# A three-layer decoder on one core: biases of the first two tiles on TensorE, the other two put off, adapters from two tables, twelve of sixteen parts by squares from the fifth batch

## The chip, the cores and the metric

The kernel runs on one core of a Trainium2 chip. The metric is the device time of one execution in microseconds (us). Five engines work beside one another, each with its own queue that it runs in order: PE (TensorE, matrix multiplies and transposes), DVE (VectorE), ACT (ScalarE), POOL (GpSimd) and SP (SyncE, which here only issues DMAs).

## The reference

`x` is 8 batches of 512 rows of 256 values; everything is 32-bit floating point. Three layers follow one another, each ended by `x = layernorm(x + layer(x))`.

```python
# 1: linear attention (16 heads of 16) and an MLP
xn = layer_norm(x, ln1_w, ln1_b)
q, k, v = (xn @ w.T + b for w, b in ((q_w, q_b), (k_w, k_b), (v_w, v_b)))   # split over heads
q, k = elu(q) + 1, elu(k) + 1
kv = einsum('bhnd,bhne->bnde', k, v)             # per row n: a sum over the 16 heads
attn = einsum('bhnd,bnde->bhne', q, kv) / einsum('bhnd,bnd->bhn', q, k.sum(axis=1))[..., None]
x = x + attn @ o_w.T + o_b
x = x + gelu(layer_norm(x, ln2_w, ln2_b) @ fc_w.T + fc_b) @ proj_w.T + proj_b      # hidden width 1024
# 2: cross-attention, 16 heads of 64, over 512 rows of context of width 128
attn = softmax((x @ Wq) @ (ctx @ Wk).T / 8);  out = (attn @ (ctx @ Wv)) @ Wo + bo
# 3: a base layer and one of 8 adapters for each batch
losses = mean((relu(x @ W_enc[n] + b_enc[n]) @ W_dec[n] + b_dec[n] - x) ** 2)      # per batch and n
a = connected_idx[argmin(losses)]
out = x @ W_base + b_base + relu(x @ W_down[a] + b_down[a]) @ W_up[a] + b_up[a]
```

The sums `kv` and `attn` of layer 1 run over heads or over 16 features within one row, so they are no matrix multiplies: they are elementwise products and reductions.

## The kernel before, in words

**A planner writes the order.** The program first lists tasks (`task(engine, took, due, emit, reads, writes, ...)`). Each has an engine, an estimated duration in ns, a due time, and values that it reads and writes. `others=` names engines that may take it instead after a wait; `two=True` says that on DVE it reads two SBUF operands, and `alone()` then makes it exclude POOL's elementwise work in the plan. `play()` then goes through a planned time and, at each step, gives every free engine the ready task with the earliest due time whose buffers are free (`rooms`, `roomy`). The result is a fixed instruction order for PE, ACT, DVE, POOL and for SP's DMAs. Due times are in units of PACE = 3200 ns; batch b's cross-attention is due from 64·b PACE on. A planned time orders the work and sets no wait on the chip, where semaphores alone hold an instruction back.

**Layer 1** (`linear_attention`, `tile_attention`) goes by tiles of 128 rows, four to a batch (c = 0 to 3). For each tile: norm (DVE statistics L388, POOL power L402, DVE scale L410), transposes and `turn_tile` (scale and bias, DVE L460), projection to q, k and v on PE (`project`, L511), the bias of q and k added by DVE in PSUM (L519), that of v on its way to SBUF (L527), exponential on ACT (L523, L524), k and q (DVE L537, L549). Then four products k·v of 128x1088 (L559, POOL, or DVE), each summed by DVE (L568); four products q·kv (L582, POOL, or DVE) and their sums (L591); division, output projection (L632), second norm. Batch 0 runs its MLP tile by tile (`mlp_by_tiles`, L712 and L687); later batches run layer 1 some two batches ahead of their cross-attention, in `WINDOWS` of due times. `FIRST` holds the due times of batch 0's four tiles.

**Layer 2** (`cross_attention`, `attend`) goes by pairs of heads (8) and halves of the rows (2): 16 parts to a batch. Batch 0 does its eight pairs for tiles 0 and 1 first, and for tiles 2 and 3 after that, so that it can start when two tiles are through. A part has four score tiles of 128x512 (L847), maxima (DVE L854), exponential (ACT L862), scaling by 1/sum (POOL L873 or ACT L871), transposition of the probabilities, and the weighting of v (`weigh`, L929). The transposition has two forms. By PE: 16 transposes of 128x128 into PSUM (L893) and four copies out (ACT L372 or DVE L374). By squares, for the parts listed in `BLOCKED`: DVE transposes each 128x512 tile in 32x32 squares (L883, four to a part) into `blk`, and SP issues 16 DMAs (`place`, L913) that move the squares within SBUF into `pT`. There is one buffer of its own for `blk` and one for `pT`, and one more of each that lies over two of layer 1's four product buffers (`prods`). Probabilities before transposition have seven buffers (`p`).

**Layer 3** (`ffn`): base bias added to x by POOL (L377 with `bbase`, four tiles), encoders L973 and decoders L1076, squared errors on ACT (L1093), the adapter chosen by nine small DVE operations (`choose`, L1102 to L1115), five indirect DMAs issued by POOL (L1001: two for W_down, one each for b_down, W_up, b_up), the middle product (L1019), relu with bias (L1023), then by tiles: b_up added by POOL (L377 with `bu`), base and up products in one PSUM group (L1038, L1039), added by DVE (L1045), norm, output by SP (L1060, L1066).

## Time and profile before

| | |
|---|---|
| median of 3 runs | 1677.8 us (1677.01 to 1680.26) |
| the profiled execution: its time, and its span from first to last instruction | 1677.12 us, 1675.3 us |
| busy: PE, DVE, ACT, POOL | 1569.5, 1320.5, 1084.0, 1075.2 us |
| mean granted PE clock over the span | 0.972 |
| first scores of cross-attention (L847) | 103.73 us after the start |
| parts transposed by squares | 61 of 128 (976 DMAs of L913) |

The profile's times are counted from the first instruction of the span. A group's line gives engine, operation, tiles written and read, how many, busy time and mean time of one. A window's line gives the busy time of each engine in that stretch, the PE clock granted, and what the DMA engines did. In a timeline an entry shows start and duration, and in brackets how long the engine had been idle and what it had waited for.

### The profile page before, as it was taken

The numbers are of one execution on the slowest core, as the hardware profiler recorded it, in microseconds if no ns is written. First come the engines' busy times: TensorE is split into PE (matmuls) and PEld (weight loads), VectorE is DVE, ScalarE is ACT, GpSimd is POOL, SyncE is SP. The second block draws the span as 40 slices with busy tenths as digits, with TensorE's granted clock in tenths as the row PEclk, the third lists the DMA queues.
The fourth block names the chain that finished last, engine by engine and source line by source line (L and its number), as shares of the span: only waits on it lengthen the run. The fifth ranks groups of instructions, "written<-read, shape, count | busy, mean of one in ns | idle before, by whom it ended". The sixth has DMA issues, their size and how long they took to land.

```text
span 1675.3 us, 23902 instructions
## 1 busy us (share of the span) xinstructions
PE 1569.5 (94%) x7856; PEld 935.4 (56%) x7856; DVE 1320.5 (79%) x2261; ACT 1084.0 (65%) x2359; POOL 1075.2 (64%) x881
## 2 busy tenths in 40 slices
PE   4489999999999999999998999989999899999996
PEld 2366666664665555565565565655566554654562
DVE  7987886798889898979976797868969566776554
ACT  1147776678676787678756677657766567646643
POOL 6955886686678697669565794758938241544243
PEclk8689999999999999999999999999999999999998
DMA  8000000022113211221113121221112322333301
GB/s 267 1 1 1 1 1 0 8 54 58 33 34 88 52 26 38 53 75 51 48 29 89 46 52 30 59 79 28 51 35 55 88 72 68 80 100 91 91 7 32
DMA packets 159003, 86.68 MB, mean 52 GB/s; under 512 B 18336, under 2 KB 156192, under 8 KB 158880
## 3 DMA queue, kind: packets, MB, share of 16 engines
q1 hardware_dynamic: 157472, 83.06, 18.4%
q0 software_dynamic: 1408, 2.10, 0.6%
q8 instruction: 63, 1.03, 0.3%
q14 instruction: 60, 0.49, 0.1%
HBM read 16.93 MB, written 4.19 MB: 13 GB/s over the span
## 4 chain that ended last, share of the span: by engine, by line
PE 74%; DVE 10%; SPq 4%; issue 3%; ACT 3%; POOL 3%; DMA 2%; POOLq 0%; DVEq 0%; ACTq 0%
PE sc L847 12%; PE bank L929 12%; PE bank L687 7%; PE bank L662 6%; PE bank L945 5%; PE bank L793 5%; PE bank L893 5%; PE bank L511 4%; SPq L913 4%; PE bank L973 3%; PE bank L800 3%; PE bank L1076 3%; PE bank L809 3%; DVE o L591 2%; ACT p L862 2%
## 5 line engine op out<-in xcount | busy, mean ns | idle before, releaser
L862 ACT ACTIVATE p<-sc,nmax 128x512 f32<-128x512 f32 x512 | 348.1, 689 | 111.3 <-DVE nmax L854 88.6
L873 POOL TENSOR_SCALAR p<-p,rinv 128x512 f32<-128x512 f32 x284 | 204.5, 731 | 325.6 <-DVE rinv L867 316.5
L854 DVE TENSOR_REDUCE nmax<-sc 128x2 f32<-128x1024 f32 x256 | 304.9, 1213 | 82.7 <-PE sc L847 82.0
L559 POOL TENSOR_TENSOR prods<-k,v 128x1088 f32<-128x1088 f32 x119 | 297.5, 2523 | 59.8 <-DVE k L537 32.6
L847 PE MATMUL sc<-kT,qT 64*128 64x512 f32 x1024 | 265.5, 627 | 5.5 <-ACT p L862 4.3
L582 POOL TENSOR_TENSOR prods<-q,kv 128x1088 f32<-128x1088 f32 x95 | 237.4, 2519 | 37.3 <-DVE kv L568 25.6
L568 DVE TENSOR_REDUCE kv<-prods 128x68 f32<-128x1088 f32 x128 | 162.3, 1273 | 10.9 <-POOL prods L559 10.5
L893 PEld LDWEIGHTS bank<-ident,p 128*128 128x128 f32 x1072 | 121.7, 141 | 80.4 <-issue 45.7
L591 DVE TENSOR_REDUCE o<-prods 128x68 f32<-128x1088 f32 x128 | 160.6, 1271 | 4.5 <-POOL prods L582 4.5
L871 ACT ACTIVATE p<-p,rinv 128x512 f32<-128x512 f32 x228 | 155.5, 730 | 3.2 <-DVE rinv L867 2.7
L893 PE MATMUL bank<-ident,p 128*128 128x128 f32 x1072 | 150.3, 277 | 2.6 <-ACT qT L804 1.1
L847 PEld LDWEIGHTS sc<-kT,qT 64*128 64x128 f32 x1024 | 88.7, 190 | 109.6 <-issue 77.2
L929 PE MATMUL bank<-prods,v 128*64 128x256 f32 x1008 | 127.9, 397 | 16.0 <-DMA prods<-blk 14.7
L883 DVE STREAM_TRANSPOSE blk<-p 128x512 f32<-128x512 f32 x184 | 121.9, 689 | 25.7 <-POOL p L873 11.0
L929 PE MATMUL bank<-pT,v 128*64 128x256 f32 x1040 | 128.0, 388 | 4.0 <-DMA prods<-prods 2.1
L793 PE MATMUL bank<-x1T,Wq 128*128 128x512 f32 (+1 forms) x288 | 124.1, 554 | 1.0 <-DVE x L1045 0.5
L945 PE MATMUL bank<-Wo,oT 128*128 128x256 f32 x512 | 121.1, 382 | 0.0
L687 PE MATMUL bank<-projT,h 128*128 128x256 f32 x512 | 119.1, 383 | 1.3 <-ACT h L723 1.3
L687 PEld LDWEIGHTS bank<-projT,h 128*128 128x128 f32 x512 | 95.3, 190 | 26.0 <-issue 9.2
L945 PEld LDWEIGHTS bank<-Wo,oT 128*128 128x128 f32 x512 | 94.8, 190 | 26.5 <-issue 12.1
L929 PEld LDWEIGHTS bank<-prods,v 128*64 128x64 f32 x1008 | 70.2, 141 | 70.6 <-issue 29.6
L372 ACT COPY oT<-bank 128x256 f32<-128x256 f32 x100 | 37.2, 372 | 110.2 <-PE bank L929 109.7
(142 smaller groups left out, 2859.1 us busy)
## 6 DMA issues: line engine op xcount, KB each, us to landing
prods<-blk SPq DMA_DIRECT2D x480, 64.0 KB, 2.1
pT<-blk SPq DMA_DIRECT2D x256, 64.0 KB, 2.1
prods<-prods SPq DMA_DIRECT2D x176, 64.0 KB, 2.1
pT<-prods SPq DMA_DIRECT2D x64, 64.0 KB, 2.1
x<-in_x SPq DMA_DIRECT2D x7, 512.0 KB, 6.5
out<-x SPq DMA_DIRECT2D x7, 512.0 KB, 3.4
ctx<-in_ctxT SPq DMA_DIRECT2D x8, 256.0 KB, 3.1
fcT<-in_fcT SPq DMA_DIRECT2D x1, 1024.0 KB
```

The costliest lines, as they stand in the source:

```text
L559: (nc.gpsimd if e == "pool" else nc.vector).tensor_tensor(pr.t.rearrange("p (d e h) -> p d e h", d=DSPLIT, h=H1), k.t[:, s : s + DSPLIT, : ...
L582: (nc.gpsimd if e == "pool" else nc.vector).tensor_tensor(pr.t.rearrange("p (h e d) -> p h e d", h=DSPLIT, d=D1), q.t[:, s : s + DSPLIT, : ...
L591: nc.vector.tensor_reduce(o.t[:, s : s + DSPLIT, :], pr.t.rearrange("p (h e d) -> p h e d", h=DSPLIT, d=D1), AX.X, ALU.add)
L687: nc.tensor.matmul(ps.t[:, :C], of(f, c), projT[:, f, :], start=f == fs[0], stop=f == fs[-1])
L793: nc.tensor.matmul(ps_q.t[:, :n], Wq[:, kc, cols], x1T.t[:, kc, rows], start=kc == 0, stop=kc == KC - 1)
L847: nc.tensor.matmul(ps.t[:, i, :], qT.t[rows, c * P : (c + 1) * P], kT.t[rows, :], start=True, stop=True)
L854: lambda: nc.vector.tensor_reduce(nmax.t, ps.t, AX.X, ALU.max, negate=True), [(ps, 0)], [(nmax, 0)],
L862: lambda i=i, p=p: nc.scalar.activation(p.t, ps.t[:, i, :], AF.Exp, bias=nmax.t[:, i : i + 1], accum_out=ssum.t[:, i : i + 1]),
L873: nc.gpsimd.tensor_scalar(p.t, p.t, rinv.t[:, i : i + 1], 1.0, ALU.mult, ALU.mult)
L893: nc.tensor.transpose(bank.t[:, m * P : (m + 1) * P], p.t[:, m * P : (m + 1) * P], ident)
L929: nc.tensor.matmul(to, v2.t[:, m, cols], of, start=m == 0, stop=m == NT - 1)
L945: nc.tensor.matmul(ps.t[:, :C], oT.t[:, c * P : (c + 1) * P], Wo[:, pr, :], start=pr == prs[0], stop=pr == prs[-1])
```

## The change

Four edits go together.

1. *Opening.* For tiles 0 and 1 of batch 0 (`EARLY`) the biases of q, k and v come from a third matmul of one row (`ones` times `bqkv`) in the same PSUM group; the DVE bias adds are gone, and ACT copies v. Their `kv` lies in a PSUM tile of the scores' room instead of SBUF, and their q·kv products are DVE's alone and no longer exclude POOL in the plan. Tiles 2 and 3 get later due times (`FIRST`), and their k·v products may not be planned before 65 and 75 us (`HOLD`). `turn_tile` goes to ACT first. The bias loads are issued behind the three weight loads.
2. *Adapters.* The host lays W_down, b_down, W_up, b_up and the base bias in two tables, so two gathers stand for five. Two rows that are always one carry b_up and the base bias through the up product; the eight POOL additions of each batch are gone. `choose` has seven operations instead of nine. In the last batch the base products are a task of their own, due ahead of the choice, two tiles to a bank.
3. *Room.* `p` has eight buffers; `bu`, `bbase` and `bd` are gone.
4. *Squares.* `BLOCKED` takes both halves of every second pair from batch index 4 on (before: 6), which makes 12 of 16 parts in batches 4 and 5 instead of 8. Batches 1 to 3, 6 and 7 keep theirs.

```diff
-FIRST = (-80, -60, -40, -20)
+FIRST = (-80, -70, -28, -6)
...
-    b: [(pr, half) for pr in range(NPAIR) for half in range(2) if half or b > 5 and pr % 2] for b in range(1, B)
+    b: [(pr, half) for pr in range(NPAIR) for half in range(2) if half or b > 3 and pr % 2] for b in range(1, B)
...
+EARLY = (0, 1)
+HOLD = {(0, 2): 65000.0, (0, 3): 75000.0}
...
-    room("p", 7, [P, S])
+    room("p", 8, [P, S])
...
+    for i, n in enumerate("qkv"):
         nc.sync.dma_start(out=bqkv[:, i * C : (i + 1) * C], in_=t[f"b{n}"].partition_broadcast(P))
...
+    row_base = const.tile([P, 2], F32, name="row_base")
+    row_step = const.tile([P, 2], F32, name="row_step")
+    nc.gpsimd.iota(row_base, [[0, 2]], base=0, channel_multiplier=1, allow_small_or_imprecise_dtypes=True)
+    for j, step in enumerate((P, UP)):
...
+    wd = const.tile([P, KC * P + 1], F32, name="wd")
...
-        def put():
+        def put(e):
             for kc in range(KC):
-                nc.vector.tensor_scalar(
...
+                to, of, wk, bk = dst.t[:, kc, cols], ps.t[:, kc * P : (kc + 1) * P], w[:, kc : kc + 1], b[:, kc : kc + 1]
+                if e == "act":
+                    nc.scalar.activation(to, of, AF.Identity, bias=bk, scale=wk)
+                else:
+                    nc.vector.tensor_scalar(to, of, wk, bk, ALU.mult, ALU.add)
+
+        task("act", 560, due + 1, put, [(ps, 0)], [(dst, (kc, c)) for kc in range(KC)], names, others=[("dve", 720, 300)])
...
+        early = b == 0 and c in EARLY
+
         def project(ps, lo, hi):
             for kc in range(KC):
                 nc.tensor.matmul(
-                    ps.t[:, : hi - lo], xnT.t[:, kc, cols], wqkv[:, kc, lo:hi], start=kc == 0, stop=kc == KC - 1
-                )
-
-        task("pe", mm(512, 2), due, lambda: project(qk, 0, 2 * C), chunks(xnT, [c]), [(qk, 0)], ("wqkv",), "full")
-        task("pe", mm(256, 2), due + 1, lambda: project(ps_v, 2 * C, 3 * C), chunks(xnT, [c]), [(ps_v, 0)], ("wqkv",), "full", holds=[v])
...
+            if early:
+                nc.tensor.matmul(ps.t[:, : hi - lo], ones[0:1, :], bqkv[0:1, lo:hi], start=False, stop=True)
+
+        needs = ("wqkv", "bqkv") if early else ("wqkv",)
+        task("pe", mm(512, 2 + early), due, lambda: project(qk, 0, 2 * C), chunks(xnT, [c]), [(qk, 0)], needs, "full")
+        task("pe", mm(256, 2 + early), due + 1, lambda: project(ps_v, 2 * C, 3 * C), chunks(xnT, [c]), [(ps_v, 0)], needs, "full", holds=[v])
...
-        task(
-            "dve", 595, due + 0.2 * step,
...
+        if early:
+            task(
+                "act", 380, due + 0.1 * step,
+                lambda: nc.scalar.copy(
+                    v.t[:, 0:D1, :].rearrange("p e h -> p h e"), ps_v.t[:, :C].rearrange("p (h e) -> p h e", h=H1)
+                ),
+                [(ps_v, 0)], [(v, 0)],
+            )
...
-        kv, o = Val("kv"), Val("o")
+        kv, o = Val("sc" if early else "kv"), Val("o")
+
+        def kv_of():
+            return kv.t[:, 0, : E1 * D1].rearrange("p (e d) -> p e d", d=D1) if early else kv.t
+
...
-            task("pool", 2490, due + (1 + 1.2 * i) * step, kv_product, [(k, 0), (v, 0)], [(pr, 0)], holds=[kv],
+            task("pool", 2490, due + (1 + 1.2 * i) * step, kv_product, [(k, 0), (v, 0)], [(pr, 0)], holds=[kv], after=HOLD.get((b, c), 0.0),
                  others=[("dve", 1340, 500 if b == 0 else 5000)], two=True)
...
+            keys = [(q, 0)] + [(kv, j) for j in range(0, D1, DSPLIT)]
+            if early:
+                task("dve", 1340, due + (7 + 1.5 * i) * step, lambda p=o_product: p("dve"), keys, [(pr, 0)], holds=[o])
+            else:
+                task(
+                    "pool", 2490, due + (7 + 1.5 * i) * step, o_product, keys, [(pr, 0)], holds=[o],
+                    others=[("dve", 1340, 0 if b == 0 else 3000)], two=True,
+                )
...
-        long = end - begin
+        long, final = end - begin, b == B - 1
         turn(x2T, x2, begin)
-        for c in range(NT):
-            task(
-                "pool", 728, begin + (0.1 + 0.05 * c) * long,
-                lambda e, c=c: add(e, x2.t[:, c, :], x2.t[:, c, :], bbase),
-                [(x2, c)], [(x2, c)], ("bbase",), others=[("dve", 420, 4000)], two=True,
-            )
...
-        task("dve", 1900, begin + 0.61 * long, lambda: rows.append(choose(b, ps_l.t)), [(ps_l, 0)], [(chosen, 0)])
+        task("dve", 1500, begin + 0.61 * long, lambda: rows.append(choose(b, ps_l.t)), [(ps_l, 0)], [(chosen, 0)])
...
-        for kc in range(KC):
-            task("pool", 1000, due, gather(lambda kc=kc: wd[:, kc, :R], Wdown_rows, every, slice(kc, kc + 1)),
-                 [(chosen, 0)], [(v_wd, kc)], slack=2000)
-        task("pool", 1000, due + 1, gather(lambda: bd[:R], bdown_rows, slice(0, R), slice(2, 3)), [(chosen, 0)], [(v_bd, 0)], slack=2000)
-        task("pool", 1000, due + 2, gather(lambda: wu[:R], Wup_rows, slice(0, R), slice(2, 3)), [(chosen, 0)], [(v_wu, 0)], slack=2000)
-        task("pool", 1000, due + 3, gather(lambda: bu.t, t["bup"], every, slice(3, 4)), [(chosen, 0)], [(bu, 0)], slack=2000)
+        task("pool", 1000, due, gather(lambda: wd, down_rows, slice(0, P), slice(0, 1)), [(chosen, 0)], [(v_wd, 0)], slack=2000)
+        task("pool", 1000, due + 1, gather(lambda: wu[:UP], up_rows, slice(0, UP), slice(1, 2)), [(chosen, 0)], [(v_wu, 0)], slack=2000)
...
+        task(
+            "act", 686, begin + 0.82 * long, lambda: nc.scalar.activation(mid.t, ps_m.t, AF.Relu, bias=wd[:, KC * P :]),
+            [(ps_m, 0), (v_wd, 0)], [(mid, 0)],
...
-        for c in range(NT):
-            task(
-                "pool", 723, begin + 0.8 * long + c,
-                lambda e, c=c: add(e, x2.t[:, c, :], x2.t[:, c, :], bu.t),
-                [(x2, c), (bu, 0)], [(x2, c)], others=[("dve", 420, 4000)], two=True,
-            )
+
+        for cs in ((0, 1), (2, 3)) if final else ((0,), (1,), (2,), (3,)):
...
+            def base(cs=cs, ps=ps):
+                for n, c in enumerate(cs):
+                    for kc in range(KC):
+                        nc.tensor.matmul(
+                            ps.t[:, n * C : (n + 1) * C], x2T.t[:, kc, c * P : (c + 1) * P], Wbase[:, kc, :],
+                            start=kc == 0 and n == 0, stop=False,
+                        )
+
+            def up(cs=cs, ps=ps):
+                for n, c in enumerate(cs):
+                    nc.tensor.matmul(
+                        ps.t[:, n * C : (n + 1) * C], mid.t[:, c * P : (c + 1) * P], wu, start=False, stop=c == cs[-1]
+                    )
+
+            due = begin + (0.86 + 0.03 * cs[-1]) * long
+            if final:
+                task("pe", mm(256, 4), begin + (0.6 + 0.01 * cs[-1]) * long, base, chunks(x2T, cs), [(ps, 0)], ("Wbase",), "full")
+                task("pe", mm(256, 2), due, up, [(mid, 0), (v_wu, 0)], [(ps, 0)], kind="full")
+            else:
+                task("pe", mm(256, 3), due, lambda f=base, g=up: (f(), g()), chunks(x2T, cs) + [(mid, 0), (v_wu, 0)],
+                     [(ps, 0)], ("Wbase",), "full")
+            for n, c in enumerate(cs):
+                task(
+                    "dve", 416, due + 0.02 * long,
+                    lambda n=n, c=c, ps=ps: nc.vector.tensor_tensor(
+                        x2.t[:, c, :], x2.t[:, c, :], ps.t[:, n * C : (n + 1) * C], ALU.add
+                    ),
+                    [(ps, 0), (x2, c)], [(x2, c)],
+                )
+                norm.stats(c, due + 0.03 * long)
         if final:
...
-        loss = small.tile([P, NA], F32, tag="loss", name=f"loss_{b}")
-        nc.vector.tensor_copy(loss, ps[:, :NA])
         least = small.tile([P, 1], F32, tag="least", name=f"least_{b}")
-        nc.vector.tensor_reduce(least, loss, AX.X, ALU.min)
+        nc.vector.tensor_reduce(least, ps[:, :NA], AX.X, ALU.min)
         pick = small.tile([P, NA], F32, tag="pick", name=f"pick_{b}")
-        nc.vector.tensor_scalar(pick, loss, least, -float(NA), ALU.is_equal, ALU.mult)
+        nc.vector.tensor_scalar(pick, ps[:, :NA], least, -float(NA), ALU.is_equal, ALU.mult)
...
-        nc.vector.tensor_scalar(first, first, float(NA), None, ALU.add)
-        nc.vector.scalar_tensor_tensor(pick, iota_a, first, cidx, ALU.is_equal, ALU.mult)
+        nc.vector.scalar_tensor_tensor(pick, iota_low, first, cidx, ALU.is_equal, ALU.mult)
...
+    down = np.zeros((NA, P, KC * P + 1), np.float32)
+    for kc in range(KC):
+        down[:, :, kc * P : kc * P + R] = a["ffn_W_down"][:, kc * P : (kc + 1) * P]
+    down[:, :R, -1] = a["ffn_b_down"]
+    down[:, R:UP, -1] = 1.0
+    b_base = np.broadcast_to(a["ffn_b_base"], (NA, 1, C))
+    up = np.concatenate([a["ffn_W_up"], a["ffn_b_up"][:, None], b_base], axis=1)
```

## The prediction

> **What bounds the kernel now.** I read the page's head and its slices first, then windows over the stages, and then the timeline where a window was not full. From the page:
>
> ```profile
> span 1675.3 us, 23902 instructions
> PE 1569.5 (94%) x7856; PEld 935.4 (56%) x7856; DVE 1320.5 (79%) x2261; ACT 1084.0 (65%) x2359; POOL 1075.2 (64%) x881
> ...
> PE   4489999999999999999998999989999899999996
> ```
>
> PE is the bound from the third slice on; the first two slices and the last are not full. Two sets of windows (PE, PEld, DVE, ACT, POOL, PE clock) show how full, the first over the opening and its end, the second over the stages of batches 3 and 4:
>
> ```profile
> 13.50:63.40 49.90, 24.93 (x91) 17.46 (x90) 45.69 (x53) 10.16 (x21) 41.12 (x19) 0.66 0.55 183
> 63.40:82.30 18.90, 4.62 (x21) 3.21 (x19) 18.59 (x26) 1.07 (x4) 18.21 (x13) 0.69 0.00 0
> 82.30:103.70 21.40, 13.82 (x62) 11.04 (x62) 19.63 (x26) 3.30 (x11) 12.89 (x10) 0.74 0.00 0
> 103.70:150.00 46.30, 46.06 (x268) 32.55 (x270) 32.90 (x71) 35.64 (x79) 26.57 (x26) 0.99 0.00 1
> ```
> ```profile
> 697.00:895.00 198.00, 196.43 (x979) 116.17 (x977) 167.39 (x294) 140.00 (x297) 145.01 (x119) 1.00 0.21 56
> 895.00:1093.00 198.00, 192.13 (x949) 112.83 (x950) 161.08 (x279) 136.66 (x290) 136.99 (x108) 0.98 0.20 51
> ```
>
> Until 103.7 us DVE is full and PE half idle, at a clock near 0.7; from there PE is full and DVE has 15 to 20% left. So a microsecond is worth itself where it brings the first scores (103.73) nearer, or where it leaves PE's list later. What PE lacks in batch 4 is one stall, which comes back at 1116.7 and 1314.1:
>
> ```profile
> 897.10 0.68 DVE L883 STREAM_TRANSPOSE blk<-p 128x512 f32<-128x512 f32 x1
> ...
> 905.47 0.39 SPq L1066 DMA_DIRECT2D out<-x  x1
> 906.28 10.27 SPq L913 DMA_DIRECT2D prods<-blk  x16
> ...
> 918.32 3.68 PE L929 MATMUL bank<-prods,v 128*64 128x256 f32 x16 [4.73 <-DMA prods<-blk]
> ```
>
> The squares were ready at 897.8, but SP stood at `out`, whose rows POOL finished (L414) at 905.4. PE then waited 4.73 and ran cold: L929 3.68 for a usual 1.95, the scores behind it 3.03 for 1.92. That is 4.73 + 1.73 + 1.11 = 7.6 us; the other two come to 7.7 and 7.9, together 23.
>
> **Edit 1, the opening.** Tile 1's attention ends at 63.44 (`at`), its first scores at 103.73: 40.3 us. The chain between, without queueing: `at`, transpose, copy, L632, add, statistics, power, scale, transpose, turn = 5.9; L712 to the start of L687 6.9, L687 3.7; add, statistics, power, scale, transpose, copy, Wq 2.07, qT = 5.7; with 17 hand-overs of 0.15 it is 24.7. The other 15.6 are DVE, busy with tiles 2 and 3 (`xhat` started at 80.51 and its power L402 had ended at 73.5).
>
> Work of DVE that stands before tile 1's `at`, from k at 16.1: 8 kv sums at 1.27, 8 o products at 1.28 and 8 o sums at 1.27 are 30.6; two or three k·v products 3.5; k and q of tile 1, divisions, tile 0's add and norm 4; some of tiles 2 and 3 (bias, v, k, q) 3. Sum 41, so `at` near 57 and first scores near 57 + 24.7 = 82: 22 earlier. The earliest is 16.1 + 30.6 + 24.7 = 71, the latest as before, 103. The bias rows add matmuls of 512 and 256 columns at 0.86 and 0.43 (pieces of L511), 2.6 for two tiles, on a PE that is half idle; they take the place of L519 (0.70) and L527 (0.59) on DVE. Ahead of k they cost 0.86 and save 0.70: nothing. The v copy on ACT (0.4) has an ACT that is busy 10 of 50 us; without that cover it costs 0.4 twice. The kv sums now write PSUM and the o products read it: L519 (PSUM and SBUF, 512) has 0.17 over its columns at 0.96 per ns, L582 (SBUF) 0.15, so nothing to 0.2 for eight. The bias loads move behind three weight loads of 0.47 issue on SP: k's and v's weights come sooner, the last bias no later. `turn_tile` on ACT takes 0.6 for 0.72.
>
> What is late next: DVE. Tiles 2 and 3 need about 2 x 21 us, of which some 12 are done by 82; the other 30 run beside attention, which takes 62% of DVE (12.43 of 20 at 120 to 140). Paying 30 from the 38% takes 80 us, and batch 0's first half lasts about as long, so it fits, but tile 2's due times stand ahead of the first scores. I give back 7: net 15. If none of it hid, 22 − 30 = −8; if all hid and the scores came at 71, 32. Range −8 to 32; 15 is nearer the upper half, by the 62%.
>
> **Edit 2, the adapters.** In mid-kernel the eight POOL additions (0.72) and three gathers (1.22 from one to the next) of a batch are 9.4 us of a POOL with 50 free: worth nothing by themselves, covered by L873's 316 us of waiting for `rinv`. But they lie in the chain to `out`: four `bu` additions 2.79, three gathers 3.7, two operations of `choose` 0.4 are 6.9 of the 8.5 us that SP stood. The planner's own estimate shrinks too, so its order may again put `out` first. I take 10 of the 23; ends: one stall more (−8) and all 23.
>
> At the end of the kernel the path itself has them:
>
> ```profile
> 1624.34 2.77 POOL L377 TENSOR_TENSOR x<-x,bu 128x256 f32<-128x256 f32 x4 [2.71 <-DMA bu<-in_bup,rows]
> ...
> 1627.07 1.04 POOL L402 TENSOR_TENSOR rs<-ve,neghalf 128x4 f32<-128x4 f32 x1
> ...
> 1663.92 2.79 POOL L377 TENSOR_TENSOR x<-x,bu 128x256 f32<-128x256 f32 x4 [2.64 <-DMA bu<-in_bup,rows]
> ...
> 1664.69 0.42 DVE L1045 TENSOR_TENSOR x<-x,bank 128x256 f32<-128x256 f32 x1 [9.73 <-POOL x L377]
> ```
>
> Batch 7's power stood behind batch 6's additions from 1624.1: 2.9 gone. After the choice: 0.4 of `choose`; one gather of 1 KB rows for two of 256 B, which lands later (`bu`, of such rows, took 3.52, `wd` 2.6) but is alone: about nothing; then L1045 can follow the up product (L1023 ends 1662.4, two cold L1039 0.6) at 1663.2 for 1664.69: 1.5. Base products early fill an idle PE. Sum 5; ends 1 and 8.
>
> **Edit 3, the room.** PE's scores waited 4.3 us in all for `p`: 0 to 4, taken as 0, since the squares use the buffer.
>
> **Edit 4, the squares.** Rows of batches 4 and 5 (895 to 1291):
>
> ```profile
> L883 DVE STREAM_TRANSPOSE blk<-p 128x512 f32<-128x512 f32 x57 | 38.0, 689 | 8.3 <-POOL p L873 3.8 <-DMA ctx<-in_ctxT 2.3 <-ACT qT L804 1.7
> L893 PE MATMUL bank<-ident,p 128*128 128x128 f32 x256 | 35.7, 277 | 0.0
> L372 ACT COPY pT<-bank 128x512 f32<-128x512 f32 x52 | 28.9, 592 | 9.4 <-DVE x L952 4.9 <-PE bank L893 4.3
> ```
>
> Sixteen parts by PE are 35.7, so 2.2 a part; eight parts leave PE: 17.8, from windows in which PE is full. DVE gains four L883 and loses a share of the copies (0.75 of 0.67): 2.3 a part, 9 per batch on 161 of some 190, 90%. ACT loses 1.9 a part. SP gains 4 x 10.3 per batch; its twelve parts are 124 of 190 us, and `out`, x and ctx loads queue behind them. I keep 13 of 17.8 for DVE's crowding; ends 18 and, if every new part stalled as at 918, 17.8 − 8 x 7.7 = −44.
>
> A rule speaks against this edit. The Trainium skill, VectorE: DVE Perf Modes, Rules for kernel authors, puts a full 128x128 transpose on TensorE when PSUM can take it and leaves 32x32 squares to DVE. In work done the trace agrees: four L883 (2.8) and 16 DMAs (10.3) stand against 2.2 on PE and four copies. Followed, edit 4 would charge 8 x 2.3 = 18 to DVE where I count a gain of 13, and the time would be 1666; the windows above, with PE at 196 of 198 and DVE at 167, are why I go by the rows.
>
> **Sum.** 15 + 10 + 5 + 0 + 13 = 43 off the profiled execution's 1677.1 (span 1675.3 and 1.8 around it) is 1634; the median lies 0.7 above that execution: 1635.
>
> **Rivals.**
> - *The opening's gain is given back.* DVE, not PE, paces 82 to 300 (it is at 85% from 150 to 250). For it: the debt of 30. Against: DVE falls to 67% at 250 to 300. Gain 0 there: 1650.
> - *The stalls stay and the new squares wait as well.* For it: SP's order is the planner's, and `blk` has one buffer while layer 1 holds `prods`. Stalls 0, squares 6: 15 + 5 + 6 = 26, 1652.
> - *All of it arrives.* First scores at 80 and nothing given back, no stall left: 24 + 23 + 7 + 17 = 71, 1607. For it: PE keeps 46 of 46.3 full once scores run. Against: 90% DVE in batches 4 and 5.
> - *Slower, by `blk` alone.* A square part holds `blk` some 18 us (four L883 spread over 6 to 8, then 10.3 of DMAs): twelve are 216 of 190 us in the stretches where `prods` is taken, and PE waits 7.7 per new part: 15 + 10 + 5 + 17.8 − 61.6 = −14, 1692. It decides from seven of the eight parts on. Against it: batch 6 runs twelve parts with one such stall, though without layer 1 beside it.
> - *The change does not do what it says*: DVE, not the order of its tiles, sets the first scores, and the squares give DVE what they take from PE. Gains of some 5 at the end against as much of new waits, 1677.
>
> **How the numbers follow.** Chances: forecast 0.44, opening given back 0.16, stalls stay 0.17, all 0.13, slower 0.07, nothing 0.03. Faster than 0.2% (3.4 us, about what a measurement here can tell) is the first four: 0.90; within 0.03; slower 0.07. The range leaves out the last two and half of the case *all*: 1608 to 1665, the upper end being 1652 with another 13 of squares and opening lost.
>
> **What would show it.** First L847 at 78 to 88, PE at least 90% full from there to 150. The bias add of L519 30 times for 32, gathers 16 for 40, no addition with `bu` or `bbase`. Transposes on PE (L893) 944 for 1072, squares (L883) 276 for 244. No wait of 5 us at L929 some 20 us into batches 4 to 6. From the last part's choice to the end 1.5 to 2 us less. Wrong if L847 starts after 95, if L929's waits for `blk` grow past 30 us, or if PE falls under 47 of 50 in batches 4 and 5.

## The result, and the profile after

The changed kernel takes 1659.7 us (median, 1658.9 to 1661.2) where the kernel before takes 1677.4: a ratio of 0.9895 with a 95% interval of 0.9871 to 0.9920. The forecast was 1635, a gain of 43; the gain is 18. The profiled execution took 1659.94 us. Its page begins so, and the last line shows PE's busy tenths in 40 slices:

```profile
span 1658.1 us, 23850 instructions
PE 1561.0 (94%) x7736; PEld 919.3 (55%) x7736; DVE 1321.9 (80%) x2248; ACT 1055.4 (64%) x2318; POOL 1020.2 (62%) x821
...
PE   5579999999999999989999999999999999999995
```

PE has 8.5 us less to do and is as full as it was, 94%. The first two slices went from 4 to 5 and the third from 8 to 7. The counts are those of the change: 944 transposes by PE, and the bias addition of q and k 30 times. Windows over the opening (PE, PEld, DVE, ACT, POOL, PE clock), cut at tile 1's `at` (57.68), at the end of its MLP's second product (77.86) and at the first scores:

```profile
13.50:57.70 44.20, 24.89 (x71) 14.00 (x70) 37.24 (x44) 10.33 (x17) 25.56 (x19) 0.70 0.58 200
57.70:77.90 20.20, 18.00 (x101) 15.96 (x100) 12.33 (x24) 5.38 (x18) 11.08 (x9) 0.89 0.00 0
77.90:92.20 14.30, 2.77 (x8) 1.47 (x8) 14.27 (x15) 0.76 (x2) 12.08 (x6) 0.67 0.00 0
92.20:138.50 46.30, 42.23 (x224) 27.09 (x225) 37.41 (x65) 29.64 (x70) 29.14 (x29) 0.92 0.00 1
```

`at` came at 57.7, as forecast; the first scores at 92.18, not 82. In the last 14.3 us before them PE has 2.8 of work and DVE is full. The timeline of DVE from 70 us to the first scores:

```profile
70.31 2.69 DVE L409 SCALAR_TENSOR_TENSOR x<-x,mv,rs 128x256 f32<-128x256 f32 x1 [0.66 <-POOL rs L401]
...
75.31 3.60 DVE L580 TENSOR_TENSOR prods<-k,v 128x1088 f32<-128x1088 f32 x1
78.84 1.27 DVE L589 TENSOR_REDUCE kv<-prods 128x68 f32<-128x1088 f32 x1
80.04 0.40 DVE L717 TENSOR_TENSOR x<-x,bank 128x256 f32<-128x256 f32 x1
80.37 1.27 DVE L589 TENSOR_REDUCE kv<-prods 128x68 f32<-128x1088 f32 x1
81.56 0.41 DVE L387 BATCH_NORM_STATS2 st<-x 128x6 f32<-128x256 f32 x1
...
83.39 1.93 DVE L603 TENSOR_TENSOR prods<-q,kv 128x1088 f32<-128x1088 f32 x1
85.24 1.27 DVE L589 TENSOR_REDUCE kv<-prods 128x68 f32<-128x1088 f32 x1
86.44 1.27 DVE L612 TENSOR_REDUCE o<-prods 128x68 f32<-128x1088 f32 x1
87.63 0.81 DVE L409 SCALAR_TENSOR_TENSOR x<-x,mv,rs 128x256 f32<-128x256 f32 x1
```

Products and sums (L580, L589, L603, L612) of tile 2 stand between the steps of tile 1's last norm (L717, L387, L409). Tile 2's products were to be put off to 65 us of the plan; on the chip they began at 70.24, and tile 1 was not yet through. The norm's power on POOL (L401) stood behind one of them too.

What follows the first scores on PE, in the changed kernel and then in the kernel before:

```profile
92.19 3.78 PE L872 MATMUL sc<-kT,qT 64*128 64x512 f32 x8 [0.47 <-ACT qT L829]
...
101.77 1.13 PE L657 MATMUL bank<-woT,atT 128*128 128x256 f32 x4 [3.48 <-ACT atT L371]
```
```profile
103.73 2.53 PE L847 MATMUL sc<-kT,qT 64*128 64x512 f32 x8 [0.47 <-ACT qT L804]
```

The first eight score matmuls take 3.78 us for 2.53 (granted clock 0.50 from 92.2 to 96.1, where before had 0.78 from 103.7 to 106.3), and then PE stands 3.48 us at tile 2's output projection (L657), which waits for a copy on ACT. That copy started at 101.35, behind a table load and two exponentials of the first scores in ACT's order.

The three stalls at the starts of batches 4 to 6 are gone. One stands now at the start of batch 3 (timeline, entries of DVE, POOL, SP and PE):

```profile
698.97 0.70 DVE L908 STREAM_TRANSPOSE prods<-p 128x512 f32<-128x512 f32 x1
...
706.78 4.83 POOL L413 TENSOR_SCALAR x<-x,mv,rs 128x256 f32<-128x256 f32 x4
711.64 0.38 SPq L1091 DMA_DIRECT2D out<-x  x1
712.12 11.39 SPq L938 DMA_DIRECT2D prods<-prods  x16
725.12 3.68 PE L954 MATMUL bank<-prods,v 128*64 128x256 f32 x16 [6.10 <-DMA prods<-prods]
```

It is the old picture in another place: squares ready at 699.7, SP standing at a store whose rows POOL finishes at 711.6, PE waiting 6.1 and then running cold, that is slower than usual: L954 takes 3.68 for 1.95, at a granted clock of 0.50.

**One table for all kernels.** PE is the bound, so I split each profiled span at the first scores of every batch and subtract from each stretch the work of the matmuls begun in it, an estimate with each matmul at its back-to-back duration in these rows (0.43 us for 512 columns, in proportion for fewer, half of it where 64 rows or columns are used; 0.125 for a transpose of 128). What is left is PE's loss in us: waits, and matmuls slower than that. Each row is one profiled execution; kernels with a part left out or added come from the experiments below.

```
                       first          loss of PE in batch            last weighting
                       scores   0    1    2    3    4    5    6    7     at
before                 103.7  12.6 14.0 14.0 11.3 18.8 18.3 19.1 18.0  1617.0
before, slower chip    102.6  13.0 13.9 13.8 14.0 19.8 21.7 19.4 18.4  1623.7
opening alone           91.6  24.8 14.0 17.5 14.0 19.6 21.2 19.1 17.2  1627.2
squares alone          102.7  12.9 14.6 13.8 14.4 31.2 22.2 14.1 19.3  1616.4
tables alone           102.8  12.5 16.6 16.3 12.5 13.2 14.4 11.1 18.6  1605.0
opening, tables         90.8  21.0 16.4 16.5 12.3 13.4 14.5 11.2 18.8  1603.3
tables, room           103.1  14.1 12.3 15.0 22.5 12.7 18.2 10.3 17.2  1612.6
all but squares         91.3  19.2 12.2 15.0 23.0 12.8 18.1 10.4 17.2  1607.7
all but room            92.2  23.3 16.7 16.2 12.4 22.6 21.6 11.5 18.1  1606.8
all but opening        101.4  13.8 12.2 16.8 23.1 16.5 19.7 10.6 17.6  1602.9
changed                 92.2  19.9 12.3 14.9 23.3 17.7 18.8 10.6 17.6  1599.6
changed, later hold     82.0  28.4 13.7 13.1 25.8 22.6 17.8 10.6 15.4  1601.7
changed, POOL stores    92.1  19.9 12.2 17.9 15.3 17.2 18.2 11.0 16.0  1592.2
changed, both mends     91.3  19.2 12.2 19.5 15.3 16.3 18.7 11.3 15.7  1591.6
```

Two more profiles of the changed kernel put the last weighting at 1595.9 and 1598.8, with batch 4 at 15.7 and 18.8 and batch 7 at 16.6 and 16.1; the other batches stay within 0.8. So a difference of 2 or 3 us in one cell says little.

From before to changed, the first scores come 11.5 us sooner, and the batches lose 9.0 more: 7.3 in batch 0, 12.0 in batch 3, 8.5 less in batch 6, 1.8 less in the others. These nearly cancel. Of the 7.3 in batch 0, 6.2 lie in the first 18 us behind the first scores, where the changed kernel loses 8.0 and before 1.8: the cold scores and the wait at L657 above. Every kernel here with the opening loses 7.6 to 8.0 there, every one without it 1.8 to 2.3. The other 14.9 of the 17.4 us by which the last weighting is earlier are work that PE no longer has in the batches (128 transposes of 0.125 are 16.0). The end, from the last weighting on, takes 58.5 where it took 58.3.

### The profile page after: what moved, and what is told of

It is laid out like the page before. It is cut to its first block, busy times and chain, and to the rows that moved or that the text cites. A ratio compares the mean times of both kernels' runs of the same rounds, so it can differ in the third digit from the quotient of the medians.

```text
span 1658.1 us, 23850 instructions
## 1 busy us (share of the span) xinstructions
PE 1561.0 (94%) x7736; PEld 919.3 (55%) x7736; DVE 1321.9 (80%) x2248; ACT 1055.4 (64%) x2318; POOL 1020.2 (62%) x821
## 3 DMA queue, kind: packets, MB, share of 16 engines
q1 hardware_dynamic: 175760, 91.32, 20.6%
## 4 chain that ended last, share of the span: by engine, by line
PE 64%; DVE 17%; ACT 6%; SPq 5%; issue 4%; POOL 2%; DMA 2%; DVEq 0%; POOLq 0%; ACTq 0%
PE bank L954 10%; PE sc L872 10%; PE bank L970 5%; PE bank L687 5%; SPq L938 5%; PE bank L712 5%; PE bank L918 5%; PE bank L818 4%; DVE nmax L879 4%; PE bank L514 3%; DVE o L612 3%; PE bank L825 2%; ACT p L887 2%; PE bank L992 2%; DVE kv L589 2%
## 5 line engine op out<-in xcount | busy, mean ns | idle before, releaser
L898 POOL TENSOR_SCALAR p<-p,rinv 128x512 f32<-128x512 f32 x300 | 209.3, 710 | 294.5 <-DVE rinv L892 275.9
L580 POOL TENSOR_TENSOR prods<-k,v 128x1088 f32<-128x1088 f32 x115 | 288.9, 2533 | 72.8 <-DVE k L554 38.8
L603 POOL TENSOR_TENSOR prods<-q,kv 128x1088 f32<-128x1088 f32 x107 | 266.7, 2516 | 37.6 <-DVE kv L589 24.8
L589 DVE TENSOR_REDUCE kv<-prods 128x68 f32<-128x1088 f32 x120 | 152.3, 1272 | 17.8 <-POOL prods L580 17.5
L612 DVE TENSOR_REDUCE o<-prods 128x68 f32<-128x1088 f32 x128 | 161.3, 1270 | 4.6 <-POOL prods L603 4.5
L918 PEld LDWEIGHTS bank<-ident,p 128*128 128x128 f32 x944 | 106.4, 141 | 88.9 <-issue 48.6
L896 ACT ACTIVATE p<-p,rinv 128x512 f32<-128x512 f32 x212 | 143.8, 732 | 6.2 <-DVE rinv L892 6.2
L908 DVE STREAM_TRANSPOSE blk<-p 128x512 f32<-128x512 f32 x200 | 130.9, 687 | 17.0 <-POOL p L898 9.3
L918 PE MATMUL bank<-ident,p 128*128 128x128 f32 x944 | 134.6, 278 | 9.3 <-ACT qT L829 2.6
L954 PE MATMUL bank<-pT,v 128*64 128x256 f32 x1040 | 128.2, 389 | 5.7 <-DMA pT<-blk 2.7
L954 PE MATMUL bank<-prods,v 128*64 128x256 f32 x1008 | 124.4, 389 | 6.9 <-DMA prods<-prods 6.1
L687 PE MATMUL bank<-xT,fcT 128*128 128x512 f32 x224 | 105.9, 600 | 2.2 <-DVE x L717 1.1
L1111 DVE SCALAR_TENSOR_TENSOR h<-bank,decb,xT 128x512 f32<-128x512 f32 x128 | 88.9, 740 | 21.7 <-PE bank L1101 20.7
```

What stands on the lines that cost most here:

```text
L580: (nc.gpsimd if e == "pool" else nc.vector).tensor_tensor(pr.t.rearrange("p (d e h) -> p d e h", d=DSPLIT, h=H1), k.t[:, s : s + DSPLIT, : ...
L603: (nc.gpsimd if e == "pool" else nc.vector).tensor_tensor(pr.t.rearrange("p (h e d) -> p h e d", h=DSPLIT, d=D1), q.t[:, s : s + DSPLIT, : ...
L612: nc.vector.tensor_reduce(o.t[:, s : s + DSPLIT, :], pr.t.rearrange("p (h e d) -> p h e d", h=DSPLIT, d=D1), AX.X, ALU.add)
L898: nc.gpsimd.tensor_scalar(p.t, p.t, rinv.t[:, i : i + 1], 1.0, ALU.mult, ALU.mult)
L918: nc.tensor.transpose(bank.t[:, m * P : (m + 1) * P], p.t[:, m * P : (m + 1) * P], ident)
L954: nc.tensor.matmul(to, v2.t[:, m, cols], of, start=m == 0, stop=m == NT - 1)
```

## The experiments

Times are compared with the kernel before on the same chip. On some chips it took 1685 to 1688 us and on others 1676 to 1677, so medians are given beside ratios; the last experiment is on that. Diffs are cut to the lines that matter.

**1. Each part alone.** Before, with the opening alone, the tables alone, the squares alone:

```diff
-FIRST = (-80, -60, -40, -20)
+FIRST = (-80, -70, -28, -6)
+EARLY = (0, 1)
+HOLD = {(0, 2): 65000.0, (0, 3): 75000.0}
...
```


> The kernel before with edit 1 alone (biases by TensorE for two tiles, tiles put off, holds, loads reordered). Theory A, effects stay where the edit is: first scores at 92 us as in the changed kernel, 4 us of that left at half of batch 0, so 1674 (-4). Theory B, the planner writes another order everywhere and the order decides later: first scores still at 92, but the end anywhere from 1660 to 1685, and the stalls of batches 4 to 6 shifted to other batches. My forecast had -15 for this edit.


```diff
+    down_rows = t["down"].rearrange("n p m -> (n p) m")
+    up_rows = t["up"].rearrange("n r d -> (n r) d")
...
```


> The kernel before with edit 2 alone (two tables, base products of the last batch ahead). Theory A: the last batch's norm 3 us earlier, its choice to the end 1.7 us shorter, its decoders 5.6 us longer because the base products hold two of four banks: 0 at the end; one or more of the stalls of batches 4 to 6 gone, so -0 to -15. Theory B: the 7.7 us stalls are there in other batches, total within 5 us of before. My forecast had -15 for this edit (10 stalls, 5 end).


```diff
-    ... if half or b > 5 and pr % 2] for b in range(1, B)
+    ... if half or b > 3 and pr % 2] for b in range(1, B)
```


> The kernel before with edit 4 alone, seven buffers for p. Theory A: 17.8 us of transposes leave PE, batches 4 and 5 get 8 us shorter each less their new waits, so -8 to -16; the three stalls stay. Theory B: waits of PE at the weighting and at the scores eat more than half of it, 1670 or more. My forecast had -13.

Before took 1687.9. The opening alone took 1686.3 (0.9996, 0.9981 to 1.0011): first scores at 91.6, and by batch 1 its marks stood 1 us behind those of before. The tables alone took 1666.3 (0.9869, 0.9840 to 0.9897): the three stalls are gone, 56.2 us of loss in batches 4 to 6 became 38.7, while batches 1 to 3 lose 6.1 more; the end took 59.9 for 58.3. The squares alone took 1675.1 (0.9914, 0.9881 to 0.9947). There the stall at the start of batch 4 stayed (4.77 us), and those of batches 5 and 6 went. Against before on a slower chip, batch 4 loses 11.4 more (31.2 for 19.8): PE waits 4.1 at L793 for DVE's addition of the bias of v (L527) and then runs cold, in a stretch where DVE is 98% busy (19.56 of 20 us from 980). So a crowded DVE did cost something, and the lost stalls paid for it. The opening is the term that failed by itself.

**2. The end.** In the changed kernel the last batch's base products are made to wait for `part`, the sum that the losses are taken from:

```diff
-  ... base, chunks(x2T, cs), [(ps, 0)], ("Wbase",), "full")
+  ... base, chunks(x2T, cs) + [(part, 0)], [(ps, 0)], ("Wbase",), "full")
```


> The changed kernel, with the last batch's base products made to wait for the losses (one more value read by those two tasks), so that they can't take two of the four PSUM banks while the decoders run. Theory A (banks): the stretch from the last norm's transposes to the losses falls from 26.2 to 20.6 us, the rest stays, so 1654 (-5.5). Rival: the stretch is long because PE runs batch 6's base and up products in it, then it stays at 26 and the time at 1660.

1652.4 us (0.9797, 0.9764 to 0.9830), 5 to 7 under the changed kernel on other chips. From the last weighting to the end it takes 54.4 us for 58.5. The timeline of the changed kernel in the end, PE and DVE:

```profile
1610.63 1.04 PE L428 MATMUL bank<-ident,x 128*128 128x128 f32 x8
...
1626.45 1.99 PE L1048 MATMUL bank<-Wbase,xT 128*128 128x256 f32 x8
1629.43 1.99 PE L1048 MATMUL bank<-Wbase,xT 128*128 128x256 f32 x8
1629.53 1.41 DVE L1111 SCALAR_TENSOR_TENSOR h<-bank,decb,xT 128x512 f32<-128x512 f32 x2 [1.50 <-PE bank L1101]
1632.58 1.41 DVE L1111 SCALAR_TENSOR_TENSOR h<-bank,decb,xT 128x512 f32<-128x512 f32 x2 [1.64 <-PE bank L1101]
1636.82 0.17 DVE L1007 TENSOR_TENSOR part<-acc 128x8 f32<-128x8 f32 x1 [0.79 <-ACT h L1118]
1643.03 3.41 PE L1033 MATMUL bank<-xT,wd 128*128 128x512 f32 x4 [5.40 <-DMA wd<-in_down,rows]
```

and of the kernel with this edit:

```profile
1605.03 1.04 PE L428 MATMUL bank<-ident,x 128*128 128x128 f32 x8
...
1621.02 2.73 DVE L1111 SCALAR_TENSOR_TENSOR h<-bank,decb,xT 128x512 f32<-128x512 f32 x4 [1.22 <-PE bank L1101]
1624.38 2.73 DVE L1111 SCALAR_TENSOR_TENSOR h<-bank,decb,xT 128x512 f32<-128x512 f32 x4 [0.63 <-PE bank L1101]
1627.89 0.17 DVE L1007 TENSOR_TENSOR part<-acc 128x8 f32<-128x8 f32 x1 [0.79 <-ACT h L1118]
1628.56 6.38 PE L1048 MATMUL bank<-Wbase,xT 128*128 128x256 f32 x16
1634.77 1.88 PE L1033 MATMUL bank<-xT,wd 128*128 128x512 f32 x4
```

The base products (L1048) that the change drew forward stand among the decoders (L1101), on a PE whose timeline shows no wait from 1609 to 1632: DVE gets its error tiles in twos with waits of up to 1.6, for fours with 0.6 to 1.2. Whether it is the 3.98 us that they take on PE or the banks that they hold, this run does not separate, since it moves both. From the last norm's transposes (L428) to `part` it is now 22.9 us for 26.2; before took 20.6, so 2.3 of the 5.6 stay. In both kernels two of batch 6's base and up products (3.2 us) still run behind these transposes, where in before all four stood ahead of them, so the rival of the expectation is right in part. Behind `part` the base products lie in the wait for the gathers: the middle product (L1033) starts 0.7 later after `part`, and then takes 1.88 for 3.41.

**3. The squares in company, and the hold.** The changed kernel again; it without the squares; it with the hold of tiles 2 and 3 moved so far that tile 1 is through; it with the stores of batches 0 to 6 issued by POOL:

> The changed kernel again, on the chip of the three runs beside it, to compare them with: 0.9895 of before if chips agree.


```diff
-... b > 3 and pr % 2] for b in range(1, B)
+... b > 5 and pr % 2] for b in range(1, B)
```


> The changed kernel with edit 4 undone (batches 4 and 5 with 8 parts by squares again). The runs of one edit alone gave -22 us for the adapters and -14.5 for the squares, which both lost the stalls of batches 4 to 6. Theory A (the same stalls were counted twice): without the squares those stalls stay away, the transposes are back with 17.8 us of PE less the waits that the squares brought, so 5 to 10 us slower than the changed kernel. Theory B (the squares crowd DVE and SP so that they cost what they save): same time within 4 us, or faster.


```diff
-HOLD = {(0, 2): 65000.0, (0, 3): 75000.0}
+HOLD = {(0, 2): 78000.0, (0, 3): 88000.0}
```


> The changed kernel with the two holds at 78 and 88 us instead of 65 and 75. Theory A (tile 2's products cut into tile 1's chain): L717 follows L712 without the 2.2 us, the scale L409 follows its power, first scores at 85 for 92, and DVE's debt is larger, so that at half of batch 0 3 to 7 us are left of the 7; end 3 to 7 us earlier. Rival (DVE paces the first half whatever comes first): first scores at 85 and half of batch 0 at the same 188, end unchanged.


```diff
-                "sp", 0, end,
-                lambda: nc.sync.dma_start(out=out[b].rearrange(...), in_=x2.t), each(x2, NT), slack=4000,
+                "pool", 1000, end,
+                lambda: nc.gpsimd.dma_start(out=out[b].rearrange(...), in_=x2.t), each(x2, NT), slack=4000,
```


> The changed kernel with the stores of batches 0 to 6 issued by POOL, which makes the rows, so that SP never waits for them. Theory A (SP stands at the store while squares are ready): the wait of 6.1 us at L954 in batch 3 and the cold clock behind it go, 6 to 9 us faster. Rival (the squares of that part come late by themselves: ready at 711 with the store at 711.6, and DMAs of 11.4 us): the wait stays, time within 3 us.

Changed again: 1657.9 us (0.9839, 0.9823 to 0.9856). Without the squares: 1669.6 (0.9910, 0.9893 to 0.9926), so they are worth 11.7 for the 13 forecast. With the later hold: 1664.0 (0.9876, 0.9860 to 0.9893), 6 us slower, although the first scores came at 81.97, the forecast's 82. Of the 10 us, batch 0 loses 8.5 more than in the changed kernel. Two of its windows:

```profile
150.00:200.00 50.00, 48.08 (x263) 32.50 (x263) 44.92 (x67) 35.38 (x80) 42.22 (x22) 1.00 0.00 1
200.00:250.00 50.00, 43.43 (x264) 28.54 (x264) 49.66 (x69) 34.58 (x79) 41.25 (x23) 1.00 0.00 1
```

The same two in the changed kernel, and after them in the kernel before:

```profile
150.00:200.00 50.00, 47.21 (x274) 31.95 (x272) 45.73 (x68) 35.00 (x79) 42.63 (x23) 1.00 0.00 1
200.00:250.00 50.00, 49.39 (x297) 31.92 (x295) 47.53 (x68) 37.41 (x87) 44.34 (x25) 1.00 0.00 1
```
```profile
150.00:200.00 50.00, 48.79 (x284) 31.90 (x281) 42.46 (x67) 36.22 (x85) 39.74 (x26) 1.00 0.00 1
200.00:250.00 50.00, 48.41 (x294) 31.61 (x293) 42.65 (x60) 36.29 (x83) 42.01 (x26) 1.00 0.00 1
```

From 200 to 250 DVE, the fourth number behind the window, goes from 42.65 in before to 47.53 in the changed kernel and, with the later hold, to 49.66 of 50. In the changed kernel this costs PE nothing (49.39 of 50 busy, 48.41 in before); with the later hold PE drops to 43.43, and by the measure of the table it loses 9.2 there for 3.4. So the work that the opening puts off fills DVE, but PE stood by it only with the later hold. The later end comes from batches 3 and 4 (25.8 and 22.6), where PE meets two waits of 4.0 and 4.1 us for DVE that the changed kernel does not have.

The chain from `at` to the first scores, without tile 2's work in it (PE, with the later hold):

```profile
55.55 6.46 PE L737 MATMUL bank<-xT,fcT 128*128 128x128 f32 x32 [0.90 <-ACT xT L461]
61.84 0.38 PE L653 MATMUL bank<-ident,at 128*128 128x128 f32 x2
...
68.58 3.84 PE L737 MATMUL bank<-xT,fcT 128*128 128x128 f32 x32 [0.90 <-ACT xT L461]
```

`at` was done at 57.67, but PE was in tile 0's MLP (L737) and transposed it (L653) 4.2 us later; tile 1's own L737 then took 3.84, where it took 5.59 in before, and its second MLP product began at 73.22.

With the stores on POOL the kernel takes 1654.3 (0.9818, 0.9801 to 0.9834), 3.7 us less than the changed one. The stall of batch 3 is gone (timeline, SP, POOL, PE):

```profile
709.24 11.66 SPq L938 DMA_DIRECT2D prods<-blk  x16
715.45 0.89 POOL L1091 DMA_DIRECT2D out<-x  x1
722.53 1.95 PE L954 MATMUL bank<-prods,v 128*64 128x256 f32 x16 [0.59 <-DMA prods<-blk]
```

SP no longer stands at the store: the placement starts 1.8 us after its last square (707.48), where it took 12.4 in the changed kernel. The weighting waits 0.59 and runs at 1.95. Batch 3 loses 8.0 less by the table, batch 2 3.0 more.

**4. Does the opening cost in company?** Without the squares the changed kernel was slower (1669.6) than the tables alone (1666.3), so I took the opening to cost some 5 us beside the rest. The changed kernel without the opening; with both mends (experiment 2's and the stores by POOL); with both mends and without the opening:

> The changed kernel with the opening of before (bias additions and turned tiles as they were), the tables, the room and the squares kept. Theory A (the earlier opening is paid back through VectorE, and its rearranged tiles cost the later batches some): first scores near 103 us, but the end 4 to 7 us sooner than the changed kernel, which stood at 0.984 of before on a chip like this: ratio 0.979 to 0.982. Theory B (the opening is worth its forecast and something else loses it): 8 to 15 us later than the changed kernel, ratio 0.989 to 0.993. If the opening is worth nothing: within 2 us of the changed kernel, ratio 0.983 to 0.985.

> The changed kernel with the last batch's base products held behind the losses' banks and the stores of batches 0 to 6 issued by POOL. Taken alone the two gave 5.5 and 3.7 us. If they are independent (one lies in the tail, one at the start of batch 3): 9 us under the changed kernel, ratio 0.978 to 0.979. If the stall of batch 3 only moves again: no better than the tail mend alone, 0.980 to 0.981.

> As the one with both mends, with the opening of before. Theory A: the sum of the opening's cost (4 to 7 us) and of the mends (9 us): 14 us under the changed kernel, ratio 0.974 to 0.977, the fastest of all. Theory B (the opening is worth its forecast): 8 us or more slower than with both mends, ratio 0.983 or above.

That theory fell. Without the opening: 1667.4 us (0.9957, 0.9941 to 0.9974). With both mends: 1650.2 (0.9857, 0.9839 to 0.9876). With both and without the opening: 1658.5 (0.9896, 0.9880 to 0.9913). With both mends, on one chip, the opening is worth 8.4 us. The mends are worth 8.8 without the opening (1667.4 to 1658.5), near the 9 that were expected of their sum, and the kernel with both is the fastest of all, 26.0 us under before.

**5. What the eighth probability tile does.** The room for one more tile was costed at nothing. Changed without it; tables and room; opening and tables; the changed kernel on the same chip:

```diff
-    room("p", 8, [P, S])
+    room("p", 7, [P, S])
```


> The changed kernel without the eighth probability tile. Theory C (the eighth tile lets the placements run ahead into the waiting store, and so brings the new stall of batch 3): the stall of 6 us is gone, 4 to 6 us under the changed kernel on the same chip. Theory D (the eighth tile frees VectorE and POOL from waiting and is worth something): 3 us or more over the changed kernel. Room worth nothing, as forecast: within 2 us of it.

> The tables and the eighth tile alone. The tables alone took 1666 us, the tables, the tile and the opening 1670. Theory C: 3 to 6 us over the tables alone, 1669 to 1672. Theory D: 1661 to 1664. With an opening that is worth 8 us without the squares as well, 1677, beyond before itself; by an opening that is worth nothing without the squares, 1670.

> The opening and the tables, without the eighth tile and the squares. If the opening is worth its 8 us as soon as the three stalls are gone: 1658. If it is worth something only together with the squares: 1664 to 1668. Theory C: 4 to 6 us under the kernel with opening, tables and tile (1670), that is 1664 to 1666; theory D: above 1670.

> The changed kernel again, so that the three others are compared with it on the same chip: 1657 to 1661 us, as on the two chips so far, whatever before takes here.

Before took 1685.7 here. Without the room: 1666.6 (0.9878, 0.9860 to 0.9895). Tables and room: 1675.5 (0.9939, 0.9917 to 0.9962). Opening and tables: 1666.7 (0.9892, 0.9872 to 0.9912). Changed: 1657.6 (0.9828, 0.9811 to 0.9844). So neither theory, C or D, holds by itself, and the table shows why: beside the tables the room gains 4 us in batch 1 in every kernel that has it (16.4 to 16.7 without, 12.2 to 12.3 with), brings the stall of batch 3 (12.3 to 12.5 without, 22.5 to 23.3 with), and is what the squares live on. With it the squares add 4.9 and 0.7 us of loss in batches 4 and 5 to the 16 that they spare PE; without it 9.2 and 7.1, and nothing is left (1666.7 and 1666.6). The opening, too, needs the room: beside the tables it is worth 0, beside tables and room 6 (1675.5 to 1669.6). In batch 0 PE loses 7.6 to 8.6 from 200 to 250 us in the kernels with opening and tables but without the room (a wait of 2.8 at L514 among it), and 3.1 to 3.4 in those with it. Windows over batches 4 and 5, of the kernel without the room:

```profile
905.00:1095.00 190.00, 181.58 (x882) 100.72 (x880) 161.96 (x269) 133.87 (x283) 123.55 (x92) 0.99 0.26 69
1095.00:1290.00 195.00, 185.83 (x894) 105.85 (x893) 170.40 (x289) 132.98 (x284) 131.99 (x104) 1.00 0.30 77
```

and of the changed kernel:

```profile
905.00:1095.00 190.00, 185.34 (x904) 104.91 (x903) 166.12 (x275) 125.89 (x275) 128.58 (x100) 1.00 0.27 70
1095.00:1290.00 195.00, 189.65 (x910) 107.82 (x910) 168.93 (x303) 132.06 (x284) 140.66 (x108) 1.00 0.30 78
```

PE is 3.8 us less busy in each window without the room. Its waits there are of 1 to 3 us each, for many releasers, so which one the room removes is not settled. No run has the room without the tables.

**6. Why before differs from chip to chip.** The tables again, and the kernel before on each of two chips:

> The two tables alone, a second time. Their gain was 22 us on a chip where before took 1688. If the kernel with the tables is as steady from chip to chip as the changed one: 1664 to 1668 us again, so a gain of about 11 us where before takes 1677 and of 20 where it takes 1686; the forecast for this part was 15. If before and this kernel move together: 22 us under before wherever it is.

> The kernel before, for its profile on the chip of these runs: ratio 1.000 with a few tenths of a thousandth either way. On two chips before took 1686 to 1688 us where it took 1677 on the first, and the changed kernel 1658 to 1660 on both. If the difference lies in the three stalls at the starts of batches 4 to 6 (23 us on the first chip), they are longer here by 8 to 10 us in all; if it lies elsewhere, the marks of the batches drift apart evenly from the first batch on.

> The kernel before, for a profile. Where it takes 1677: marks and stalls as in the first profile. Where it takes 1686: the stalls at the starts of batches 4 to 6 (7.6, 7.7 and 7.9 us in the first profile) are longer by 8 to 10 us in all, if it is they that differ; if all stages are longer alike, it is not they.

The tables alone took 1665.2 (0.9880, 0.9863 to 0.9896), steady. Before took 1677.0 on one chip (1.0003, 0.9991 to 1.0015) and 1685.3 on the other (1.0002, 0.9991 to 1.0013). Set side by side at equal work of PE, the second is 2.9 us ahead until 888 us and then loses 1.6, 2.2, 1.9 and 1.7 in batches 3 to 6: not in the stalls, which are as long on both (PE waits 4.7, 5.1 and 5.0 against 4.7, 5.3 and 4.9), but in steps of some 3 (1.7 in batch 6) at the adapter's base product (L1038), in part made good within some 40 us. Timeline of the slower one there:

```profile
1086.92 0.37 ACT L372 COPY oT<-bank 128x256 f32<-128x256 f32 x1 [3.32 <-PE bank L628]
...
1091.16 1.13 PE L1038 MATMUL bank<-Wbase,xT 128*128 128x256 f32 x4 [1.83 <-ACT h L1023]
```

and of the faster one:

```profile
1085.05 0.37 ACT L372 COPY oT<-bank 128x256 f32<-128x256 f32 x1
...
1089.75 1.03 PE L1038 MATMUL bank<-Wbase,xT 128*128 128x256 f32 x4
```

An ACT copy waits 3.32 us in the one and not in the other; relu (L1023) stands behind it in ACT's order, and the base products behind relu. What held the copy the trace does not say. So the change is worth 18 us where before takes 1677, and 28 where it takes 1686, since its own time hardly moves (1657.6 to 1659.7 in three comparisons).

## Why the prediction was right or wrong

The sign was right, and the time lies in the range, 5 us from its upper end; the gain was less than half of the forecast's. The steps that failed are the opening's 15, the base products that were to fill an idle PE, and the room, put at nothing. Taken in the order tables, opening, room, squares, against 1677 (another order shares it out otherwise: tables 11 to 12, room −9 to −10, squares 8, opening 8):

- **Edit 1, the opening: forecast 15, measured 0** beside the tables (1665.2 and 1666.3 against 1666.7), 0 alone, and 8 in the whole kernel. This is the step that failed most, in two of its numbers. The first scores came 11.5 earlier, not 22: from `at` to them it took 34.5 us, above all since tile 2's work stands in that chain on DVE, and I had let it run free although I had written that tile 2's due times stand ahead of the first scores. Without that work (the later hold) it is 24.9 us from 57.05 to 81.97, the forecast's 24.7, but by luck: `at` waits 4.2 us for PE, which the sum had at nothing, and in return tile 1's MLP needs 4.6 us to the start of its second product for 6.9 in the sum, and Wq 1.13 for 2.07. And 7 given back was meant for a gain of 22. In the changed kernel 7.3 of 11.5 went in batch 0, beside the tables 8.5 of 12.0, and with the scores at 82 the kernel ended 6 us later. My reason for the 7, DVE's debt, was not what took it: 6.2 of the 7.3 went in the first 18 us, to matmuls at a low granted clock and one wait behind ACT, which the sum does not have. "It fits" took the 38% from the emptiest 20 us that I had looked at behind the first scores (12.43 busy from 120 to 140; before's DVE was at 85% from 150 to 250). It held in the changed kernel, where DVE came to 95% (200 to 250 us) and PE lost nothing by it, and failed with the later hold, at 99%. The rival *the opening's gain is given back* had the number; its mechanism, that DVE paces, is seen with the later hold alone.
- **Edit 2, the three stalls: forecast 10, measured 11.5** (1677 to 1665 or 1666, with the end at 0). The gain has another make-up: all three stalls went, 17.5 us by the table, and batches 1 to 3 lost 6.1 with the new order.
- **Edit 2, the end: forecast 5, measured 0.** From the losses to the end it takes 21.3 for 23.0, near the 1.9 forecast, and the norm before comes 3.7 sooner; but "base products early fill an idle PE" was wrong. PE was not idle among the decoders, and the stretch from that norm to the losses grew by 5.6. Experiment 2 gives 3.3 of these back, and 0.9 behind the losses.
- **Edit 3, the room: forecast 0, measured 3 lost without the squares (9 without the opening too) and 9 gained with them.** The range I gave it, 0 to 4, looked only at PE's direct waits for `p`. The planner writes another order with eight tiles, and one `out` of that order stands ahead of the placements of batch 3. I had named this as the way in which stalls could stay, and sought them only in batches 4 to 6.
- **Edit 4, the squares: forecast 13, measured 11.7** (without the room 0). The transposes that left PE, 17.8 us of busy time in my sum, are 16.0 by the table. The waits that the lower end of its range and the rivals of 1652 and 1692 rest on did not come: PE's weighting waited 2.7 us for placements from `blk`, under the bound of 30, and the 6.1 in batch 3 are the room's.

Terms so measured are 11.5 + 0 − 3 + 11.7 = 20, with 17.7 measured as a whole. Of the signs named beforehand, `at` at 57, the counts, the missing waits at batches 4 to 6 and the 1.7 us at the end came true; the first scores, at 92, missed 78 to 88, and PE is 93% full from there to 150, in the 90 that was asked. That sign says little of what went wrong, since cold matmuls count as busy: 3.90 of 3.90 us from 92.2 to 96.1, at a clock of 0.50.

## What to carry to other kernels

Where one engine is the bound, count its loss and its work apart, by stages: this change looks like four gains, and by the table 14.9 of the 17.4 us that stayed at the last weighting are work taken off PE, while the waits for the most part changed places. Work put off so that a chain may start sooner must be costed in the stretch into which it falls, the chain itself among it, and not by the share left in an emptier one. And where a program orders the instructions, a buffer more or a task less changes the order everywhere: look for every in-order queue in which a waiting store can stand ahead of transfers that others need, and give such a store another queue.

## What was not expected

- The kernel before differs by 8 to 12 us (0.5 to 0.7%) between two groups of chips, the changed one by 2 over three.
- A DVE product of 128x1088 took 3.60 us at 75.31 and a scale of 128x256 2.69 at 70.31, where others took 1.27 and 0.49; POOL was in products of its own (7.53 us for three, from 70.24). Only the first stands in tile 1's chain, 2.3 of the 10 us that the first scores came late; that POOL is the cause was not tried.
- A weighting that starts after a stall takes 3.68 us for 1.95, in batch 3 as before in batches 4 to 6.
